# Boundary gathers from the input edge lists, with one short copied tail and a fixed first boundary list, in a three-layer edge convolution

## The chip, the cores and the metric

The kernel runs on one core of a Trainium2 chip. The metric is the device time of one launch in microseconds (us). The core has five engines that run beside each other and wait for one another by semaphores: TensorE (PE in the profile, PEld its weight loads), VectorE (DVE), ScalarE (ACT), GpSimd (POOL) and SyncE (SP). SP, ACT and POOL also issue DMAs; in the profile q1 is the queue of SP's DMAs, q10 that of ACT's and q0 that of POOL's, and all use the same 16 DMA engines.

## The reference

A layer norm and a relu, three edge convolutions over the same 80000 edges, and a product of all four feature sets, added to x:

```python
N, E = 2500, 80000                        # 256 features; dst is sorted
h = maximum(layernorm(x), 0)
xs = [h]
for W, b in ((W0, b0), (W1, b1), (W2, b2)):
    xi, xj = h[dst], h[src]
    m = concatenate([xi, xj - xi], -1) @ W + b
    s = segment_sum(m, dst, N)
    cnt = segment_sum(ones, dst, N)
    h = relu(s / maximum(cnt, 1)[:, None])
    xs.append(h)
return x + concatenate(xs, -1) @ Wf + bf
```

## The kernel before

The sum over edges is done as a product with a matrix of counts A, where A[s, d] is the number of edges from node s to node d. The kernel builds A once, from the edge lists, and multiplies it into the features in each layer. The nodes are taken in 20 tiles of 128 rows (ten pairs, numbered 0 to 9), and A's columns in windows of 6 destination nodes, 417 windows in 5 groups of up to 84.

**Finding the edges of a window.** Since dst is sorted, the edges of a window lie in a row. The kernel needs the place in the edge list at which each of 418 window boundaries lies; they stand in 4 blocks of 128 boundaries, one boundary on each partition. `dst` is loaded as `dst_i`, 128 rows of 625 edges. `find_first` takes the first entry of each row, `find_next` shifts it by one partition by a matmul, and `find_rows` makes `pick`, a 0/1 matrix that says in which row a boundary lies (`behind` is a step of it; `limr` holds the 512 boundaries as numbers, 6 apart). `pick_half` takes the right row of `dst_i` for each boundary by two matmuls per block, and `count_half` on ACT counts how many of the row's entries lie below the boundary. `search` makes of this the start `start_i` (six small DVE instructions), for block 0 alone and then for blocks 1 to 3 together. `get_edges` then reads, with two indirect DMAs on POOL, 256 entries of dst (`ed`) and of src (`es`) for each of a block's 128 boundaries, from that boundary's start on. A boundary's 256 entries serve the window ahead of it and the one behind it, so the first and last boundaries reach past the ends of the lists. For that the kernel copies both lists, at the start, into longer DRAM tensors `dst_e` and `src_e`, with 128 entries of `FAR` (a number above every node) ahead and behind, and gathers from those. The copies are two DMAs on ACT's queue and the borders two on SP's (lines 435 to 439).

**Counts.** `find_away` (ACT), `key_parts` and `key_high` (DVE, from `lo_i` on) make two keys of each edge, `key_turn` turns them by matmuls, `key_copy` (ACT) writes `key_m` and `key_n`. `compare` (DVE) makes 0/1 matrices `one_m` and `one_n` of the keys of 8 windows at once, `counts` (PE) multiplies them, and `take_counts` (ACT) writes the result into A's group. `degrees` and `shares` make the number of edges of a node, from `away`.

**Features.** For a pair q of tiles, `stats` (DVE) takes the layer norm's statistics of x, `spread`, `roots` and `scales` the scale and offset, `normalize` applies them on the engines that are named to it, `turn` (PE) and `take_turned` (ACT) transpose, and `product` (PE) multiplies by `W0` (names Z) and by `Wf` (names F). `split_high` (ACT) and `split_low` (DVE, writes `zl`) split the first product in two parts.

**What sets the order.** Up to the first layer, a table written by hand, `order`, lists these steps: a name is a function and its number (`Z6` is the product of pair 6 by `W0`, `st1` the statistics of pair 1, `ge0` the gather of block 0, `B5` a comparison, `Nm0` the normalization of pair 0 on DVE and ACT; `Nd` is both tiles on DVE, `Np` POOL and ACT, `Na` both on ACT, `N` both on POOL; `io` is `small_numbers`, `warm7` seven matmuls on zeros ahead of the next bank). The instructions of each engine are kept in this order, so a step that waits holds up what stands behind it on its engine. The loads of x stand in five chunks (pairs 0; 1 and 2; 3 to 5; 6 and 7; 8 and 9), all but the third on SP's queue. SP's and ACT's DMAs share eight completion semaphores in turn: a DMA waits until the one eight places ahead of it has landed. Then follow the first layer's groups, with the next group's counts woven in, and the second and third layers.

The recorded line of most instructions is 282, a helper that records them, so rows are told apart by their tiles.

Of the kernel before, what the change touches and what calls it, by code (L numbers as in the profile page):

```python
# [8 lines left out]
F32 = mybir.dt.float32  # L9
I32 = mybir.dt.int32  # L10
# [303 lines left out]
def by_windows(ctx: ExitStack, tc: tile.TileContext, x, src, dst, Ws, bs, Wf, bf, out, missing):  # L314
# [40 lines left out]
    assert W <= S - 2 and NT * S <= 256  # L355
    MORE = 4 - R % 4
# [50 lines left out]
    src_e, dst_e = (dram.tile([E + CAP, 1], I32, name=f"{z}_e") for z in ("src", "dst"))  # L407
# [26 lines left out]

    outer = pp.tile([CH, P], I32, name="outer")
    POOL.memset(outer, FAR)
    for long, of in ((dst_e, dst), (src_e, src)):
        ACTo.dma_start(long[P:P + E, :].rearrange("(p c) o -> p (c o)", p=P), of.rearrange("(p c) -> p c", p=P))
        SP.dma_start(bass.AP(tensor=long.tensor, offset=long.offset, ap=[[E + P, CH], [1, P]]), outer)
# [35 lines left out]

    lim_i = pp.tile([P, WG], I32, name="lim_i")
# [16 lines left out]
    load_b(1)  # L493
    DVE.memset(ones, 1.0)
# [3 lines left out]
    back = pp.tile([P, 2 * P], F32, name="back")  # L498
    POOL.memset(back, 0.0)
    POOL.tensor_copy(back[:, 1:P + 1], ident)  # L500
# [21 lines left out]
    limr = pp.tile([P, WG * P], F32, name="limr")  # L522
    first = pp.tile([P, 1], F32, name="first")
    after = pp.tile([P, 1], F32, name="after")
    behind = pp.tile([P, WG * P], F32, name="behind")
# [7 lines left out]
    edges = {}  # L533

# [6 lines left out]
    def limits():  # L541
        DVEo.tensor_copy(lim, lim_i)
        DVEo.tensor_copy(limr, limr_i)
        for h in range(CH):
            DVEo.tensor_scalar(below[:, h, :], lim, -1.0, 1.0 + (1 - h) * W, op0=OP.mult, op1=OP.add)
        DVEo.tensor_scalar(unlim, lim, -1.0, 0.5, op0=OP.mult, op1=OP.add)
# [35 lines left out]
    def search(i, j):  # L582
        sl = slice(i, j)
        DVEo.tensor_add(base[:, 0, sl], base[:, 0, sl], base[:, 1, sl])
        DVEo.tensor_scalar(end_f[:, sl], row[:, sl], float(R), float(HR + P * R - MORE), op0=OP.mult, op1=OP.add)
# [7 lines left out]
    def pick_starts(i, j):  # L593
# [3 lines left out]
        PEo.matmul(pe[:, :j - i], back[:, :P], end_f[:, i:j], start=True, stop=(i == 0))  # L597
        if i:
            PEo.matmul(pe[:, :j - i], back[:, P:], end_f[:, i - 1:j - 1], start=False, stop=True)
# [5 lines left out]
    def get_edges(i):  # L605

        edges[i] = [pp.tile([P, CAP], I32, name=f"e{z}{i}") for z in "sd"]
# [39 lines left out]
    def key_turn(i):  # L647
        pt = bank()
        for q, k in enumerate(parts[i]):
            for j in range(CH):  # L650
                PEo.matmul(pt[:, q * CAP + j * P:q * CAP + (j + 1) * P], k[:, j * P:(j + 1) * P], ident_b,
# [10 lines left out]
    def degrees(i):  # L662
# [17 lines left out]
        yield  # L680
        for m0 in range(0, min(P, NW + 1 - i * P), P // 2):
# [854 lines left out]
```

## Time and profile before

| what | value |
|---|---|
| time of the runs shown | median 471.64 us (471.01 to 471.9) |
| the profiled execution: time, span | 471.79 us, 470.0 us |
| granted clock of TensorE, mean | 0.99 |
| DMA moved over the span | 52.73 MB |

How to read the rows quoted below. A row of the timeline is: start (us), duration (us), engine, line, operation, tile written <- tiles read, shapes, count; in square brackets the time that the engine was idle before it and what ended that. "xN" merges N instructions that follow each other. A row of the stretches is: from and to, length, then the busy time of PE, PEld, DVE, ACT and POOL with the number of instructions, the granted clock of TensorE, the busy share of the DMA engines and GB/s. A row of a DMA queue is: packets, MB, and the time its packets took as a share of 16 engines. The layers' part of the profile looks like this, and stays as it is in all that follows:

```profile
L282 ACT CAST block<-staged 128x1008 fp32r<-128x1008 bf16 x120 | 118.0, 1031 | 16.5 <-DVE staged L282 6.9
L282 PE MATMUL bank<-block,zh 128*128 128x504 f32 (+1 forms) x200 | 83.8, 419 | 0.0
```

These are groups of like instructions, with the busy time (us), the mean of one (ns), and the idle time ahead of them.

### The profile page before, as it was taken

Reading aid. Unit: us, or ns where it says so; the run is one execution under the profiler, and the core shown is the slowest. Engines: PE = TensorE matmul, PEld = TensorE weight load, DVE = VectorE, ACT = ScalarE, POOL = GpSimd, SP = SyncE. Lnnn points to the kernel's source line nnn. Section 1 sums busy time; section 2 is a strip of 40 time slices with the busy share of each in tenths; the row PEclk is TensorE's granted clock in tenths of the full one; section 3 lists DMA queues with packets and bytes.
Section 4 is the critical chain, followed back from the end, with each engine's and each line's share of the span. In section 5 each row is a group of like instructions: output and inputs, shape, how many; then the busy total and the mean of one; then the engine's idle time right before and its main releaser. Section 6 shows DMA issues by size and latency. Waiting matters only on the chain.

```text
span 470.0 us, 7473 instructions
## 1 busy us (share of the span) xinstructions
PE 458.5 (98%) x2761; PEld 362.4 (77%) x2761; DVE 376.4 (80%) x721; ACT 312.1 (66%) x572; POOL 39.5 (8%) x65
## 2 busy tenths in 40 slices
PE   5999999999999999999999999999999999999995
PEld 2788887777777777878887877877788788688685
DVE  5889988889898873469988959876999687578795
ACT  2778769587664541387769857785787798497540
POOL 3473015200101001000000000000000000000000
PEclk9799999999999999999999999999999999999999
DMA  8510047990743708532178551010213955220014
GB/s 255 157 55 15 1 96 141 192 216 20 142 81 63 160 1 165 113 106 71 45 253 298 176 176 53 38 45 2 86 46 91 356 192 176 89 88 0 3 61 161
DMA packets 21785, 52.73 MB, mean 112 GB/s; under 512 B 1915, under 2 KB 12110, under 8 KB 21710
## 3 DMA queue, kind: packets, MB, share of 16 engines
q1 hardware_dynamic: 14318, 33.41, 21.1%
q0 software_dynamic: 5856, 16.51, 18.3%
q10 hardware_dynamic: 1568, 2.27, 1.6%
q8 instruction: 23, 0.38, 0.3%
q14 instruction: 20, 0.16, 0.1%
HBM read 36.72 MB, written 16.10 MB: 112 GB/s over the span
## 4 chain that ended last, share of the span: by engine, by line
PE 90%; ACT 3%; DVE 2%; issue 1%; DMA 1%; SPq 0%; POOL 0%; ACTq 0%; POOLq 0%; DVEq 0%
PE bank L282 84%; PE pz L282 6%; DMA acc<-in_x_dram 1%; ACT junk L282 1%; ACT a L282 1%; PE turned L282 1%; ACT hT L282 0%; ACT acc L282 0%; DVE one_m L282 0%; DVE own_h L282 0%; DVE one_n L282 0%; ACT zh L282 0%; DVE st L282 0%; DVE pick L282 0%; ACT away L282 0%
## 5 line engine op out<-in xcount | busy, mean ns | idle before, releaser
L282 ACT CAST block<-staged 128x1008 fp32r<-128x1008 bf16 x120 | 118.0, 1031 | 16.5 <-DVE staged L282 6.9
L282 PE MATMUL bank<-block,zh 128*128 128x504 f32 (+1 forms) x200 | 83.8, 419 | 0.0
L282 PE MATMUL bank<-a,zh 128*128 128x504 f32 (+1 forms) x200 | 81.9, 409 | 0.0
L282 PE MATMUL bank<-a,zl 128*128 128x504 f32 (+1 forms) x200 | 77.9, 390 | 0.0
L282 PE MATMUL bank<-block,zl 128*128 128x504 f32 (+1 forms) x200 | 77.3, 387 | 0.0
L282 ACT CAST a<-bank 128x480 fp32r<-128x480 f32 (+1 forms) x105 | 54.0, 561 | 32.4 <-PE bank L282 30.6
L282 DVE TENSOR_TENSOR one_m<-iota_m,key_m 128x2048 bf16<-128x2048 bf16 (+2 forms) x55 | 63.9, 1162 | 8.2 <-PE bank L282 7.9
L282 PE MATMUL bank<-block,sh 128*128 128x504 f32 x160 | 68.9, 430 | 0.0
L282 PE MATMUL bank<-block,staged 128*128 128x512 f32 (+1 forms) x288 | 62.8, 369 | 0.0
L282 PE MATMUL bank<-block,sl 128*128 128x504 f32 x160 | 62.6, 391 | 0.0
L282 PEld LDWEIGHTS bank<-block,staged 128*128 128x128 f32 x288 | 49.4, 188 | 10.1 <-issue 0.7
L282 DVE TENSOR_TENSOR block<-staged 128x1008 fp32r<-128x1008 bf16 x40 | 46.9, 1204 | 5.2 <-PE bank L282 3.9
L282 PEld LDWEIGHTS bank<-block,zh 128*128 128x128 f32 x200 | 37.6, 188 | 10.9 <-issue 2.5
L282 PEld LDWEIGHTS bank<-block,zl 128*128 128x128 f32 x200 | 37.6, 188 | 10.7 <-issue 3.2
L282 PEld LDWEIGHTS bank<-a,zh 128*128 128x128 f32 x200 | 37.9, 189 | 6.5 <-issue 0.2
L282 PEld LDWEIGHTS bank<-a,zl 128*128 128x128 f32 x200 | 37.8, 189 | 6.4 <-issue 0.2
L282 DVE TENSOR_TENSOR one_n<-iota_n,key_n 128x640 bf16<-128x640 bf16 (+2 forms) x110 | 42.4, 426 | 0.0
L282 PEld LDWEIGHTS <-one_m 128*128 128x128 bf16 x834 | 31.4, 98 | 13.9 <-issue 5.2
L282 PE MATMUL pz<-wbf,hT 128*128 128x256 f32 x160 | 40.7, 399 | 0.5 <-ACT hT L282 0.4
L282 PEld LDWEIGHTS bank<-block,sh 128*128 128x128 f32 x160 | 30.1, 188 | 10.3 <-issue 3.5
L282 PE MATMUL bank<-one_n,one_m 128*128 128x80 bf16 x834 | 37.6, 196 | 0.2
L282 PEld LDWEIGHTS bank<-block,sl 128*128 128x128 f32 x160 | 30.1, 188 | 9.4 <-issue 3.7
(172 smaller groups left out, 631.4 us busy)
## 6 DMA issues: line engine op xcount, KB each, us to landing
staged<-a_dram SPq DMA_DIRECT2D x52, 504.0 KB
a_dram<-a POOLq DMA_DIRECT2D x20, 630.0 KB, 8.3
acc<-in_x_dram POOLq DMA_DIRECT2D x3, 640.0 KB
out_dram<-acc SPq DMA_DIRECT2D x5, 256.0 KB
acc<-in_x_dram SPq DMA_DIRECT2D x2, 512.0 KB
wbf<-in_L_gnn_Wf_dram SPq DMA_DIRECT2D x4, 256.0 KB
acc<-in_x_dram ACTq DMA_DIRECT2D x1, 768.0 KB
wbf<-in_L_gnn_W_dram SPq DMA_DIRECT2D x3, 256.0 KB
```

The costliest lines, as they stand in the source:

```text
L282: return self.tc.keep_in_program_order(call(*args, **kwargs))
```

## The change

The full copies of the two lists go. Blocks 0, 1 and 2 gather straight from the inputs `dst` and `src`. Only the last block gathers from `dst_e` and `src_e`, of which only the last 20000 entries and a border of 128 behind them are written. Starts are held inside what each block may read by `least` and `most`, two small constant tiles that take the place of the constants 0 and E.

Block 0 now lists its boundaries in another way: its last partition holds boundary 0, whose entries are known beforehand (a border of fixed numbers and the first 128 edges, loaded by one DMA of one row for each list), and partitions 0 to 126 hold boundaries 1 to 127. So its gather has 127 partitions, and the matmuls that put the boundaries in order read `back_b` or `back` with a shift in block 0. `limr` in f32 goes; `find_rows` compares with the integer tile. The table `order` is another one.

```diff
-    lim = const.tile([P, WG], F32, name="lim")
-    back_b = const.tile([P, 2 * P], BF16, name="back_b")
+    back_b = const.tile([P, 2 * P + 1], BF16, name="back_b")
-    src_e, dst_e = (dram.tile([E + CAP, 1], I32, name=f"{z}_e") for z in ("src", "dst"))
+    TAIL = P // 4 * R
+    src_e, dst_e = (dram.tile([E + P, 1], I32, name=f"{z}_e") for z in ("src", "dst"))
-    outer = pp.tile([CH, P], I32, name="outer")
-    POOL.memset(outer, FAR)
-    for long, of in ((dst_e, dst), (src_e, src)):
-        ACTo.dma_start(long[P:P + E, :].rearrange("(p c) o -> p (c o)", p=P), of.rearrange("(p c) -> p c", p=P))
-        SP.dma_start(bass.AP(tensor=long.tensor, offset=long.offset, ap=[[E + P, CH], [1, P]]), outer)
...
-    POOLo.iota(lim_i, pattern=[[P * W, WG]], base=0, channel_multiplier=W)
+    POOLo.iota(line_i[:, 0:1], pattern=[[0, 1]], base=W, channel_multiplier=W)
+    POOLo.iota(lim_i[:, 1:], pattern=[[P * W, WG - 1]], base=P * W, channel_multiplier=W)
     POOLo.iota(limr_i, pattern=[[W, WG * P]], base=0, channel_multiplier=0)
+    POOLo.iota(limr_i[:, :P], pattern=[[W, P]], base=W, channel_multiplier=0)
+    POOLo.memset(limr_i[:, P - 1:P], 0)
...
+    outer = pp.tile([1, P], I32, name="outer")
+    POOL.memset(outer, FAR)
+    for k, (of, long, fill) in enumerate(((src, src_e, 0), (dst, dst_e, FAR))):
+        POOL.memset(edges[0][k][P - P // 4:, :P], fill)
+        SP.dma_start(edges[0][k][P - 1:, P:], of[0:P].rearrange("(o c) -> o c", o=1))
+        SP.dma_start(long[E - TAIL:E, :].rearrange("(p c) o -> p (c o)", c=R), of[E - TAIL:E].rearrange("(p c) -> p c", c=R))
+        SP.dma_start(long[E:, :].rearrange("c o -> o c"), outer)
...
+    POOL.memset(least[:, 1:], 0.0)
+    POOL.memset(least[:, WG - 1:], float(E - TAIL))
+    POOL.memset(most[:, :WG - 1], float(E - CAP))
+    POOL.memset(most[:, WG - 1:], float(E - P))
...
-        DVEo.tensor_copy(lim, lim_i)
-        DVEo.tensor_copy(limr, limr_i)
+        DVEo.scalar_tensor_tensor(lim_i[:, 0:1], line_i, float(P * W), line_i, op0=OP.is_lt, op1=OP.mult)
...
-        DVEo.tensor_scalar(behind, limr, after, None, op0=OP.is_gt)
-        DVEo.scalar_tensor_tensor(pick, limr, first, behind, op0=OP.is_gt, op1=OP.subtract)
+        DVEo.tensor_scalar(behind, limr_i, after, None, op0=OP.is_gt)
+        DVEo.scalar_tensor_tensor(pick, limr_i, first, behind, op0=OP.is_gt, op1=OP.subtract)
...
-        DVEo.tensor_scalar(end_f[:, sl], end_f[:, sl], float(E), 0.0, op0=OP.min, op1=OP.max)
-        DVEo.tensor_copy(start_i[:, sl], end_f[:, sl])
+        DVEo.tensor_tensor(end_f[:, sl], end_f[:, sl], most[:, sl], op=OP.min)
+        DVEo.tensor_tensor(start_i[:, sl], end_f[:, sl], least[:, sl], op=OP.max)
...
-        for t, of in ((ed, dst_e), (es, src_e)):
+        n = P - (i == 0)
+        for t, of in ((ed, dst_e if i == WG - 1 else dst.rearrange("(e o) -> e o", o=1)),
+                      (es, src_e if i == WG - 1 else src.rearrange("(e o) -> e o", o=1))):
             POOLo.indirect_dma_start(
-                out=t, out_offset=None, in_=of,
-                in_offset=bass.IndirectOffsetOnAxis(ap=start_i[:, i:i + 1], axis=0))
+                out=t[:n, :], out_offset=None, in_=of,
+                in_offset=bass.IndirectOffsetOnAxis(ap=start_i[:n, i:i + 1], axis=0))
...
-        warm7 lim io first next dstr st0 rs0 sq0 pick sc0 warm8 Nm0 pk00 sg00 pk01 st1 T0 pk11 R0 sg01 st2 rs1 sq1 Z0
+        warm7 lim first next dstr st0 io rs0 pick warm8 st1 sq0 sc0 Nd0 pk01 pk00 sg01 sg00 st4 T0 pk11 R0 rs1 sq1 pk30
```

On SyncE, at the program's start, `acc` is the tile that x is loaded into, `wbf` and `wt` are weights, `outer` the border. Before:

```order
L439 DMA dst_e<-outer 2x128
L439 DMA src_e<-outer 2x128
L282 DMA acc<-in_x_dram 128x2x256
L282 DMA acc<-in_x_dram 128x4x256
L282 DMA wbf<-in_L_gnn_W_dram 128x2x256
```

And after the change, with the rows that follow the loads of x and the weights:

```order
L282 DMA acc<-in_x_dram 128x2x256
L282 DMA acc<-in_x_dram 128x4x256
L282 DMA wbf<-in_L_gnn_W_dram 128x2x256
L282 DMA acc<-in_x_dram 128x4x256
L282 DMA wbf<-in_L_gnn_Wf_dram 128x2x256
L282 DMA acc<-in_x_dram 128x3x256
L282 DMA acc<-in_x_dram 68x256
L282 DMA wt<-in_L_gnn_W_dram 128x2x256
L498 DMA es_160<-in_src_dram 1x128
L489 DMA brow<-in_L_gnn_b_dram 1x256 x2
L499 DMA src_e<-in_src_dram 16x1250
```

The loads of x move to the head of SyncE's queue, and everything for the edge lists stands behind them. On ScalarE's queue the two copies that stood between `dst_i` and x's third chunk are gone.

On VectorE, from the first statistics (`st`, of the tiles in `acc`) to the start numbers of block 0 (`base`, `end_f`), before:

```order
L282 BN_STATS st<-acc 128x6 x2
L282 BN_AGGR mv<-st 128x2 x2
L282 TENSOR_SCALAR rs<-mv 128x2
L282 TENSOR_TENSOR after<-bank,after 128x1
L282 TENSOR_SCALAR behind<-limr,after 128x512
L282 SCALAR_TENSOR_TENSOR pick<-limr,first,behind 128x512
L282 RECIPROCAL rs<-rs 128x2
L282 SCALAR_TENSOR_TENSOR off<-mv,rs 128x2
L282 TENSOR_SCALAR acc<-acc,rs,off 128x256
L282 BN_STATS st<-acc 128x6 x2
L282 BN_AGGR mv<-st 128x2 x2
```

After the change:

```order
L282 CAST iota_m<-im_i 128x128
L282 CAST iota_n<-im_i 128x20x6
L282 CAST nc__102<-nc_i 128x8
L282 TENSOR_SCALAR rs<-mv 128x2
L282 TENSOR_TENSOR after<-bank,after 128x1
L282 TENSOR_SCALAR behind<-limr_i,after 128x512
L282 SCALAR_TENSOR_TENSOR pick<-limr_i,first,behind 128x512
L282 BN_STATS st<-acc 128x6 x2
L282 BN_AGGR mv<-st 128x2 x2
L282 RECIPROCAL rs<-rs 128x2
L282 SCALAR_TENSOR_TENSOR off<-mv,rs 128x2
L282 TENSOR_SCALAR acc<-acc,rs,off 128x256 x2
```

Three small casts now stand between the first statistics and `pick`, and a second pair's statistics and a second normalization stand ahead of the first transposes.

On GpSimd, around the first gather (`ed` and `es` are the gathered lists), before:

```order
L501 CAST back_b<-back 128x256
L282 DMA ed_303<-dst_e,start_i 128x256
L282 DMA es_302<-src_e,start_i 128x256
L282 TENSOR_SCALAR acc<-acc,rs,off 128x256 x6
L282 DMA ed_446<-dst_e,start_i 128x256
```

After the change:

```order
L542 MEMSET least 128x1
L282 TENSOR_SCALAR acc<-acc,rs,off 128x256
L282 DMA ed_161<-in_dst_dram,start_i 127x256
L282 DMA es_160<-in_src_dram,start_i 127x256
L282 TENSOR_SCALAR acc<-acc,rs,off 128x256 x5
L282 DMA ed_163<-in_dst_dram,start_i 128x256
```

One normalization moves ahead of the gather, and the gather reads the inputs with 127 partitions.

More of the change, by code (lines that the diff above doesn't have):

```diff
@@ L493, in by_windows @@
     load_b(1)
+    edges = {i: [pp.tile([P, CAP], I32, name=f"e{z}{i}") for z in "sd"] for i in range(WG)}
+    outer = pp.tile([1, P], I32, name="outer")
[5 more added lines that the diff above has]
+        SP.dma_start(long[E:, :].rearrange("c o -> o c"), outer)
     DVE.memset(ones, 1.0)
@@ L497, in by_windows @@
     POOL.tensor_copy(ident_b, ident)
-    back = pp.tile([P, 2 * P], F32, name="back")
-    POOL.memset(back, 0.0)
-    POOL.tensor_copy(back[:, 1:P + 1], ident)
+    back = pp.tile([P, 2 * P + 1], F32, name="back")
+    POOL.memset(back[:, 0:1], 0.0)
+    POOL.tensor_copy(back[:, 1:].rearrange("p (k n) -> p k n", k=2), ident.unsqueeze(1).to_broadcast([P, 2, P]))
     POOL.tensor_copy(back_b, back)
@@ L517, in warmed @@
         return to
-    limr = pp.tile([P, WG * P], F32, name="limr")
     first = pp.tile([P, 1], F32, name="first")
     after = pp.tile([P, 1], F32, name="after")
-    behind = pp.tile([P, WG * P], F32, name="behind")
+    behind = pp.tile([P, WG * P], BF16, name="behind")
     pick = pp.tile([P, WG * P], F32R, name="pick")
@@ L532, in by_windows @@
     start_i = pp.tile([P, WG], I32, name="start_i")
-    edges = {}
+    least = pp.tile([P, WG], F32, name="least")
+    most = pp.tile([P, WG], F32, name="most")
+    POOL.memset(least[:, 1:], 0.0)
+    POOL.memset(least[:, WG - 1:], float(E - TAIL))
+    POOL.memset(most[:, :WG - 1], float(E - CAP))
+    POOL.memset(most[:, WG - 1:], float(E - P))
     def small_numbers():
@@ L596, in pick_starts @@
         ends_before.append(pe)
[L597 to L599 removed]
+        PEo.matmul(pe[:, :j - i], back[:, 0 if i else P:][:, :P], end_f[:, i:j], start=True, stop=(i == 0), skip_group_check=True)
+        for k in range(i, j) if i else ():
+            PEo.matmul(pe[0:1, k - i:k - i + 1], back[:, P - (k == 1):][:, :1], end_f[:, k - 1:k], start=False, stop=(k == j - 1),
+                       skip_group_check=True)
     def set_starts(i, j):
@@ L680, in degrees @@
         yield
+        here, before = (ident_b, back_b) if i else (back_b[:, P:], back_b[:, P - 1:])
         for m0 in range(0, min(P, NW + 1 - i * P), P // 2):
```

32 lines of the change are left out of this document (17 added, 15 removed).

## The prediction

> **What bounds the kernel now.** I read the page first (engines, chain), then the busy time by stretches, then the timeline of the first 65 us, and last the DMA queues of the first 12 us.
>
> ```profile
> span 470.0 us, 7473 instructions
> PE 458.5 (98%) x2761; PEld 362.4 (77%) x2761; DVE 376.4 (80%) x721; ACT 312.1 (66%) x572; POOL 39.5 (8%) x65
> 0.00:10.00 10.00, 6.18 (x17) 2.40 (x17) 4.63 (x24) 2.29 (x4) 3.90 (x18) 1.00 0.79 236
> 10.00:20.00 10.00, 8.31 (x30) 6.82 (x31) 8.89 (x44) 6.41 (x21) 2.17 (x2) 0.66 0.78 248
> 20.00:30.00 10.00, 9.97 (x58) 8.82 (x57) 8.67 (x35) 6.36 (x18) 6.88 (x10) 1.00 0.10 28
> 30.00:60.00 30.00, 29.84 (x285) 25.81 (x284) 29.55 (x57) 24.68 (x56) 8.90 (x11) 1.00 0.07 19
> ```
>
> TensorE (PE) is busy for 98% of the span, and from 20 us on for all but a few tenths of each stretch. So what is left to win lies before 20 us, and a microsecond won there is kept only if PE stays full behind it. In the last row VectorE (DVE) is as full as PE, 29.55 of 30 us: it must move forward too. The third number from the right, the granted clock, is 0.66 in the second stretch. What PE waits for at the start:
>
> ```profile
> 8.31 0.75 DVE L282 BATCH_NORM_STATS2 st<-acc 128x6 f32<-128x256 f32 x2 [4.17 <-DMA acc<-in_x_dram]
> 10.10 0.75 DVE L282 SCALAR_TENSOR_TENSOR pick<-limr,first,behind 128x512 fp32r<-128x512 f32 x1
> 11.00 0.86 PE L282 MATMUL bank<-dst_r,pick 128*128 128x314 f32 x2 [3.19 <-DVE rs L282]
> 13.43 3.78 PE L282 MATMUL pz<-wbf,hT 128*128 128x256 f32 x8 [0.43 <-ACT hT L282]
> 18.50 1.89 PE L282 MATMUL pz<-wbf,hT 128*128 128x256 f32 x8
> 25.40 1.99 PE L282 MATMUL pz<-wbf,hT 128*128 128x256 f32 x8
> ```
>
> DVE idles 4.17 us until the first chunk of x has landed (8.31); the pick numbers for the edge search stand behind its statistics and are done at 10.86; PE starts at 11.00. Its first product takes 3.78 us, the next 1.89 us: half speed, then full. I use the product at 25.40 (tile pair 6, on `Wf`) as the milestone, since from there PE's list is nearly the same in both kernels.
>
> **The change part by part.** *The copies.* Who issues what, and what the queues moved:
>
> ```profile
> 0.83 0.40 ACTq L282 DMA_DIRECT2D dst_i<-in_dst_dram  x1
> 1.26 0.61 ACTq L282 DMA_DIRECT2D dst_e<-in_dst_dram  x1
> 1.91 0.60 ACTq L282 DMA_DIRECT2D src_e<-in_src_dram  x1
> 0.95 0.32 SPq L439 DMA_DIRECT2D dst_e<-outer  x1
> 1.61 1.13 SPq L282 DMA_DIRECT2D acc<-in_x_dram  x2
> q10 hardware_dynamic: 197, 0.90, 51.5%
> q1 hardware_dynamic: 244, 0.24, 12.8%
> DMA packets 749, 0.74 MB, mean 371 GB/s; under 512 B 25, under 2 KB 749, under 8 KB 749
> q10 hardware_dynamic: 111, 0.35, 124.8%
> 3.88 0.15 DVE L282 CAST first<-dst_i 128x1 f32<-128x1 int32 x1
> ```
>
> The first two queue rows are for 0 to 6 us: ScalarE's queue q10 had moved 0.90 MB, the list `dst_i` (0.32) and most of the two full copies, and SyncE's q1 only 0.24 MB. x's first chunk is 0.26 MB, so its bytes were through shortly after 6 us, and DVE saw it 2.2 us later. The row of packets is for 9.5 to 11.5 us, with both queues on rows of 1 KB: 371 GB/s. After the change q10 carries `dst_i` and then x's third chunk, q1 has x at its head, issued at 0.95 instead of 1.61. The last queue row is for 2 to 3 us, in which q10 moved what `dst_i` holds. With the first bytes at about 2.1 (an estimate from that row), `dst_i`, x's first chunk and what q10 sends beside it (0.77 MB) take 2.1 us: 4.2 us, to 4.6 if q10 has the larger share. Landing trailed the bytes by 0.9 us (`dst_i`: done by 3.0, used at 3.88) to 2.2 us. So the chunk lands between 5.1 and 6.8 us; I take 5.9, **2.4 us sooner**. The other x chunks come sooner by more than that and are never last.
>
> *DVE up to the gather.* Unit prices:
>
> ```profile
> 2.70 0.41 DVE L282 CAST iota_m<-im_i 128x128 bf16<-128x128 int32 x1
> 3.00 0.37 DVE L282 CAST iota_n<-im_i 128x120 bf16<-128x120 int32 x1
> 11.16 0.41 DVE L282 TENSOR_SCALAR acc<-acc,rs,off 128x256 f32<-128x256 f32 x1
> 15.12 0.74 DVE L282 BATCH_NORM_STATS2 st<-acc 128x6 f32<-128x256 f32 x2
> 16.00 0.72 DVE L282 BATCH_NORM_STATS2 st<-acc 128x6 f32<-128x256 f32 x2
> 21.80 0.53 DVE L282 TENSOR_SCALAR lo_i<-es 128x256 int32<-128x256 int32 x1
> ```
>
> A pair of tiles costs 0.87 us of statistics (start to start, 15.12 to 16.00). The three small casts (`io`) move from DVE's idle time to behind the first statistics: 0.3 us from start to start, 0.7 for the three. The two casts of the limits go, out of idle time: nothing. `behind` now reads int32 and writes bf16; no row shows that pair, but DVE reads int32 in 0.53 us for 256 elements at worst (`lo_i`) and f32 in 0.41, so the ends are 0 and +0.25, and I take 0. Minimum and maximum by `most` and `least` replace two instructions of the same small shape: 0. So pick ends at 5.9 + 0.87 + 0.7 + 0.2 + 1.28 = 8.95 instead of 10.86. Behind it the new order puts statistics of pair 1 (0.87), the scale (0.35) and two normalizations on DVE instead of one (0.4 each): the first pair is ready for PE at 10.95, against the 11.57 of before. Statistics of pair 4 (0.87), the start numbers (seven instructions of 0.15 us, as the small cast at 3.88: 1.05), a scale (0.35): 13.2. Five more pairs (4.35), numbers and a scale (0.6), one more pair (0.87), `zl` (0.7): `lo_i` at 19.8 instead of 21.80, with one pair and one normalization more behind it, so DVE has gained 2.0 + 0.87 + 0.4 = 3.3 us.
>
> *The gather of boundary block 0* stands behind a normalization of 0.6 us on POOL and reads the input itself; nothing of it waits for a copy any more, only for the one row that SyncE loads, which is issued behind x. It is issued at 13.85 and 15.3, against 15.01 and 16.50.
>
> ```profile
> 15.01 1.19 POOL L282 DMA_INDIRECT ed<-dst_e,start_i  x1 [10.40 <-DVE rs L282]
> 16.50 0.98 POOL L282 DMA_INDIRECT es<-src_e,start_i  x1 [0.30 <-issue]
> 32.80 1.03 POOL L282 DMA_INDIRECT ed<-dst_e,start_i  x1 [0.16 <-issue]
> 4.21 0.40 POOL L501 CAST back_b<-back 128x256 bf16<-128x256 f32 x1
> es<-src_e,start_i POOLq DMA_INDIRECT x1, 2.8
> q0 software_dynamic: 22, 0.09, 83.2%
> ```
>
> The fifth row, of the DMA issues from 15 to 20 us: 2.8 us from issue to landing for `es`, so it lands at 18.1, before `lo_i` asks for it (19.8). If that cover goes, each microsecond past 19.8 stands on DVE with the statistics of pair 3, the start numbers of three blocks and the first comparison queued behind. The copy of the last 20000 edges (0.16 MB) runs on q1 behind all of x; the last block was gathered at 32.80: 0. POOL's added memsets and iotas end about 1.2 us after the 4.6 us of before, still ahead of what reads them: 0, at worst 0.3 us where the casts of `io` share that time.
>
> *PE.* Its first real work starts at 9.0 instead of 11.00. How fast it runs is open:
>
> ```profile
> 4.87 2.94 PE L282 MATMUL bank<-idle 128*128 128x512 bf16 x8
> 7.04:10.45 3.41, 0.77 (x4) 0.15 (x2) 2.03 (x8) 0.20 (x1) 0.00 (x0) 1.00 1.02 322
> 10.45:13.86 3.41, 2.43 (x8) 1.95 (x9) 2.84 (x13) 2.23 (x8) 0.00 (x0) 0.50 1.10 352
> 13.86:17.27 3.41, 3.41 (x9) 2.66 (x9) 3.18 (x18) 1.76 (x6) 1.96 (x2) 0.50 0.86 265
> ```
>
> The granted clock fell to 0.50 at 10.45, behind a stretch in which PE was busy for 0.77 of 3.41 us (the warming matmuls end at 7.81), and came back at 17.27, behind a full stretch; 2.43 of 3.41 was not enough. After the change the first of these stretches holds the end of the warming (0.8) and two to three pick matmuls (0.5): some 1.4 of 3.41 us, which no row has. The two ends: at full clock the first product runs 11.9 to 13.65, the next pair's 14.4 to 16.15, the two behind it to 18.15 and 20.4; then normalizations on POOL (last at 21.3) and ScalarE's list are late next, and the milestone comes at 22.8, **2.6 us sooner**. At half clock up to 17.27 the first product ends at 15.65, the second at 18.85, the others at 20.85 and 23.1, the milestone at 24.3: **1.1 us sooner**. I take the middle, 1.8, since 1.4 lies between the rows that fell (0.77) and held (full).
>
> The Trainium skill (TensorE: Matmul & The Clock Gate, "What you observe" and "What's actually happening") says the clock is judged in free-running windows of 3413 ns, that a busy one frees it and an idle one halves it. The trace agrees on the length: 10.45 to 17.27 is twice 3.41. Taken at its word 1.4 us of work is not an idle window, and the gain would be 2.6 us; the row with 0.77 us, which fell, says that idle need not mean empty, and leaves 1.1 us possible.
>
> *Behind the milestone.*
>
> ```profile
> 27.85 0.68 DVE L282 TENSOR_TENSOR one_m<-iota_m,key_m 128x1024 bf16<-128x1024 bf16 x1
> ```
>
> DVE waits for the first keys, compares them from 24.8 instead of 27.85, but has 1.2 us of work to catch up that was done by then before (`sc4`, `zl` of pair 1, `lead`): it is about 1.6 us ahead at 30 us, and has 0.45 us of idle time up to 60 to give. That supports 1.8 as well. From 64 us on the order is the same.
>
> *Sum.* The profiled execution took 471.79 us, 470.0 of it span and 1.8 around it, 0.15 above the median of the runs shown (471.64). 471.79 - 1.8 = 470.0; against the median 469.8. **I forecast 469.9**, by the clock's ends 469.1 to 470.7.
>
> **The rivals.** The row of q1 up to 4 us:
>
> ```profile
> q1 hardware_dynamic: 10, 0.00, 0.4%
> ```
>
> *More than that.* x's chunk lands at 4.5, `dst_i` beside it, and the full clock holds: 2.6 + 1.4 = 4.0 us, 467.7. For it: 371 GB/s and 0.9 us of trailing. Against it: DVE is full behind 30 us.
>
> *No difference.* The chunk is late for another reason than the copies: q1 had moved next to nothing by 4 us although it was issued at 1.61. Then only the 0.66 us of earlier issue count, the casts and the statistics put ahead of the first normalization (0.7 + 0.87 + 0.4) eat them, and the milestone lies at 24.6 to 25.6: 470.9 to 472.0, say 471.6. Against it: q1 speeds up exactly as the copies end. This is also the case in which the change does not do what it says.
>
> *Slower: the gather of 127 rows.* The first block now gathers 127 partitions, a number that 16 engines can't share evenly. In the row of q0 (27.5 to 28 us) 22 packets, nearly all of 4 KB, took 83.2% of 16 engines for half a microsecond: 0.30 us each. If the 127 rows of 1 KB were worked through by one engine, that is 32 packets, 9.7 us instead of the 0.6 us of 16 engines; `es` lands at 15.3 + 2.8 + 9.1 = 27.2, `lo_i` is 7.4 us late, the keys reach PE at 29.2 and the milestone comes at 29.6, 4.2 us later than now: 476.0. It decides from a landing at about 23.4 on, since up to there the 2.6 us won and 1.1 us of slack at the milestone pay for it. Against it: block 1 to 3 show gathers of 128 rows only, nothing of 127.
>
> The Trainium skill (DMA: Bandwidth & Descriptors, "Why a DMA increments its semaphore by 16 and not by 1") states that rule: the number of engines is the largest up to 16 that divides the slowest dimension, and 127 partitions go to one; it excepts some direct copies from POOL, which get all 16. No run here shows which holds for this gather.
>
> **How the numbers follow.** Forecast 0.58, more 0.08, no difference 0.20, slower 0.14. A measurement of this kernel tells about 0.2% (0.9 us) from no change. So faster 0.66, same 0.20, slower 0.14. The range takes in the clock's ends, the better case and the case of no difference with what the casts and int32 might add: 467.7 to 472.6. It leaves out the slow gather.
>
> **What would show it.** The first statistics start at about 5.9 (below 6.8); pick ends near 9; the first product's eight matmuls take 1.7 to 1.9 us or 3.8; `lo_i` starts near 19.8 and its idle time does not name the gather; the milestone product, the first after the keys' transposes, starts at 22.8 to 24.3; q10 moves only 1.1 MB in the first 12 us. The prediction is wrong if x lands after 7.5, if DVE waits for `es` or `ed`, or if PE, though earlier at 25 us, is found waiting for comparisons between 30 and 64 us.

## The result, and the profile after

| kernel | median | against the kernel before |
|---|---|---|
| before | 471.32 us (4 runs, 470.63 to 471.9) | |
| changed | 475.80 us (4 runs, 474.93 to 476.62) | ratio 1.0094, interval [1.0077, 1.0111] |

The change makes the kernel 4.5 us slower. The forecast was 469.9 us, with 467.7 to 472.6 as its range; the time lies outside of it. It is that of the rival "the gather of 127 rows" (476.0), which had a chance of 0.14.

The page of the changed kernel, its head and its engines, and the busy time by the same stretches as before (from and to, length, busy time of PE, PEld, DVE, ACT and POOL, granted clock, DMA share, GB/s):

```profile
span 474.8 us, 7504 instructions
PE 461.0 (97%) x2765; PEld 363.1 (76%) x2765; DVE 375.0 (79%) x723; ACT 313.2 (66%) x573; POOL 40.8 (9%) x72
```

```profile
0.00:10.00 10.00, 7.98 (x22) 3.55 (x23) 6.62 (x34) 2.92 (x6) 4.12 (x27) 1.00 0.83 264
10.00:20.00 10.00, 9.46 (x47) 7.73 (x45) 8.27 (x42) 5.95 (x22) 6.84 (x5) 1.00 0.55 153
20.00:30.00 10.00, 4.40 (x16) 2.67 (x17) 3.25 (x17) 5.20 (x15) 1.79 (x4) 0.68 0.09 23
30.00:60.00 30.00, 30.00 (x256) 26.20 (x255) 27.30 (x59) 22.53 (x52) 10.43 (x12) 0.93 0.10 28
```

Compare stretch by stretch. From 10 to 20 us PE is busier than before (9.46 against 8.31) and at full clock (1.00 against 0.66): there the change works. From 20 to 30 us PE falls from 9.97 to 4.40 and VectorE from 8.67 to 3.25, and the clock is 0.68. A hole of more than 5 us has opened where before there was none.

The timeline of the changed kernel, the rows that answer to those of before:

```profile
5.01 0.75 DVE L282 BATCH_NORM_STATS2 st<-acc 128x6 f32<-128x256 f32 x2
7.07 0.75 DVE L282 SCALAR_TENSOR_TENSOR pick<-limr_i,first,behind 128x512 fp32r<-128x512 int32 x1
11.35 1.99 PE L282 MATMUL pz<-wbf,hT 128*128 128x256 f32 x8
13.37 2.80 POOL L282 DMA_INDIRECT ed<-in_dst_dram,start_i  x1 [0.21 <-issue]
16.47 2.58 POOL L282 DMA_INDIRECT es<-in_src_dram,start_i  x1 [0.30 <-issue]
24.25 0.69 ACT L282 ACTIVATE away<-ed,below 128x128 bf16<-128x128 int32 x2 [6.87 <-DMA ed<-in_dst_dram,start_i]
26.33 0.29 DVE L282 TENSOR_SCALAR lo_i<-es 128x256 int32<-128x256 int32 x1 [7.51 <-DMA es<-in_src_dram,start_i]
28.19 3.77 PE L282 MATMUL pz<-wbf,hT 128*128 128x256 f32 x8
```

Read it from the top. The statistics start 3.3 us sooner (5.01 against 8.31), `pick` ends at 7.82 instead of 10.86, and the first product starts 2.1 us sooner and takes 1.99 us instead of 3.78. Then ScalarE waits 6.87 us for `ed` and VectorE 7.51 us for `es`, the two gathers of block 0. The milestone product starts at 28.19 (before 25.40) and takes twice as long. The waits by engine, up to 30 us (total, times, longest):

```profile
DVE lo_i L282 <- DMA es<-in_src_dram,start_i: 7.5, 1, 7.5
ACT away L282 <- DMA ed<-in_dst_dram,start_i: 6.9, 1, 6.9
PEld turned L282 <- ACT acc L282: 3.4, 1, 3.4
```

The third row is how the wait reaches PE: ScalarE's normalization of `acc` stands in its order behind `away`, which waits for `ed`, and PE wants to transpose that `acc`. Behind it PE also waits for the keys, which are made from `es` (0.94 and 0.49 us at 27.12 and 28.00). The DMA issues and queue of the gathers, from 13.3 to 27 us (us from issue to landing; packets, MB, share of 16 engines), of the changed kernel:

```profile
q0 software_dynamic: 1056, 0.28, 10.7%
ed<-in_dst_dram,start_i POOLq DMA_INDIRECT x1, 10.8
es<-in_src_dram,start_i POOLq DMA_INDIRECT x1, 9.8
```

And of the kernel before, the same stretch, which also holds two gathers:

```profile
q0 software_dynamic: 96, 0.26, 6.7%
```

The same bytes went in 1056 packets instead of 96, and landed after 10 us instead of 2.8.

### The profile page after: what moved, and what is told of

It is laid out like the page before. It is cut to its first block, busy times and chain, and to the rows that moved or that the text cites. A ratio compares the mean times of both kernels' runs of the same rounds, so it can differ in the third digit from the quotient of the medians.

```text
span 474.8 us, 7504 instructions
## 1 busy us (share of the span) xinstructions
PE 461.0 (97%) x2765; PEld 363.1 (76%) x2765; DVE 375.0 (79%) x723; ACT 313.2 (66%) x573; POOL 40.8 (9%) x72
## 4 chain that ended last, share of the span: by engine, by line
PE 93%; DMA 3%; issue 1%; POOL 1%; DVE 0%; SPq 0%; POOLq 0%; DVEq 0%
PE bank L282 86%; PE pz L282 7%; DMA es<-in_src_dram,start_i 2%; DMA acc<-in_x_dram 1%; PE turned L282 1%; POOL ed L282 1%; POOL acc L282 0%; DVE acc L282 0%; SPq L282 0%; DVE kn L282 0%; DVE lo_i L282 0%; DVE away L282 0%; DVE room L282 0%; DVE es L282 0%; DVE fewer L282 0%
## 5 line engine op out<-in xcount | busy, mean ns | idle before, releaser
L282 PEld LDWEIGHTS <-one_m 128*128 128x128 bf16 x834 | 31.3, 98 | 13.3 <-issue 4.6
## 6 DMA issues: line engine op xcount, KB each, us to landing
acc<-in_x_dram POOLq DMA_DIRECT2D x3, 640.0 KB, 11.9
```

Of the source, the lines that this page charges most:

```text
L282: return self.tc.keep_in_program_order(call(*args, **kwargs))
```

## The experiments

There were two questions: is it the number 127, or something else about the new gather; and what made x late before. "Late row" below means one edit, which the other kernels build on: block 0's gather gets 128 rows again. Boundary 0's row is gathered too, from any valid start, and the fixed row is then copied over it from a small tile. The medians come from more than one chip, so kernels are best compared by their ratio to the kernel before, which ran beside each of them. A trace is of one execution.

**128 rows, the fixed row behind the gather** (g128_late_row). Against the changed kernel:

```diff
-        SP.dma_start(edges[0][k][P - 1:, P:], of[0:P].rearrange("(o c) -> o c", o=1))
+        fix.append(pp.tile([1, CAP], I32, name=f"fix{k}"))
+        SP.dma_start(fix[k][:, P:], of[0:P].rearrange("(o c) -> o c", o=1))
...
+            DVEo.tensor_scalar(start_0, start_i[:, 0:1], 0, None, op0=OP.max)
...
-        n = P - (i == 0)
+        n = P
...
+            SP.dma_start(ed[P - 1:, :], fix[1])
+            SP.dma_start(es[P - 1:, :], fix[0])
```

> The changed kernel, but block 0 gathers 128 rows again (the start of boundary 0, which lies 128 entries ahead of the list, is raised to 0 for the gather by one more small VectorE instruction), and the fixed row is written over row 127 afterwards by one DMA of one row for each list. Theory G (the gather of 127 rows is what is slow, for its number of rows): ed and es land about 3 us after their issue instead of 10.8 and 9.8, lo_i waits only for the late row, 1 to 2 us instead of 7.5, POOL spends about 1.0 to 1.2 us on each issue instead of 2.8, and the time is 468.5 to 470.5 us. Theory C (the first gather is slow because it reads the inputs while the tail copies and x's last loads run): ed and es still take 9 us or more, time 475 to 476.5. Theory O (the new order loses the time): lo_i no longer waits, but the time stays above 473.

467.52 us, ratio to the kernel before 0.9932 [0.9913, 0.9951]: faster than both kernels, and a microsecond below the range expected of the number of rows. Its timeline:

```profile
13.53 1.20 POOL L282 DMA_INDIRECT ed<-in_dst_dram,start  x1 [0.18 <-issue]
19.62 0.35 DVE L282 TENSOR_SCALAR lo_i<-es 128x256 int32<-128x256 int32 x1 [0.61 <-DMA es<-fix]
21.99 1.99 PE L282 MATMUL pz<-wbf,hT 128*128 128x256 f32 x8 [0.28 <-ACT hT L282]
```

POOL issues the gather in 1.20 us instead of 2.80, `lo_i` starts at 19.62 (the prediction had 19.8), and the milestone stands at 21.99, 3.4 us sooner than before. The row copied behind the gather costs VectorE 0.61 us of waiting (and ScalarE 0.85). Its busy time by stretches shows no hole, and full clock throughout:

```profile
10.00:20.00 10.00, 9.83 (x50) 8.22 (x49) 8.71 (x45) 7.63 (x27) 5.06 (x8) 1.00 0.53 149
20.00:30.00 10.00, 9.52 (x73) 8.03 (x71) 8.71 (x32) 7.77 (x22) 6.11 (x7) 1.00 0.23 68
30.00:60.00 30.00, 30.00 (x283) 26.42 (x281) 29.71 (x57) 24.03 (x54) 6.80 (x10) 1.00 0.08 20
```

**The same with 127 rows** (g127_late_row). Only the number goes back:

```diff
-        n = P
+        n = P - (i == 0)
```

> Like g128_late_row in everything, with the fixed row still loaded into tiles of its own and copied to partition 127, but the gather of block 0 has 127 rows again. If the number of rows is what makes the changed kernel slow: ed and es land some 10 us after they are issued, the first lo_i starts at 26 to 27 with 6.5 to 7.5 us of idle time named after es's gather, the clock falls to 0.50 between 24 and 33, and the time is 475 to 476.5. If the gain of g128_late_row came from another part of its edit (the fixed row out of the way of the gather, the start tile of its own): 467 to 468.5, and no wait for the gather.

476.98 us (475 to 476.5 was expected), ratio 1.012 [1.009, 1.0149]. The wait is back, in the waits up to 30 us:

```profile
DVE lo_i L282 <- DMA es<-in_src_dram,start: 8.1, 1, 8.1
```

So one row fewer costs 9.5 us by the medians (476.98 - 467.52, both on the same chip), 8.9 by the two ratios; and at 127 rows the late-row edit is no faster than the changed kernel (475.80), so the number of rows is what it gained by.

**Gathers of other sizes, one by one** (rows_by_number). In the kernel g128_head_copy, told of below, seven more gathers of `dst` with 128 to 64 rows, which nothing needs, each followed by a small copy on POOL that waits for it, at 42 us, where POOL and its queue are idle:

```diff
+        for n in more:
+            POOLo.indirect_dma_start(
+                out=more[n][:n, :], out_offset=None, in_=dst.rearrange("(e o) -> e o", o=1),
+                in_offset=bass.IndirectOffsetOnAxis(ap=start_i[:n, 1:2], axis=0))
+            POOLo.tensor_copy(seen[:n], more[n][:n, 0:1])
```

> The head-copy kernel with seven extra gathers of 256 entries per row from dst, for 128, 127, 126, 124, 120, 112 and 64 rows, one after the other on POOL behind its last normalization, each followed by a small POOL copy that waits for its landing; nothing uses them, and the time of this kernel says nothing but what they cost. Theory G, split by the largest divisor up to 16 (16, 1, 14, 4, 15, 16 and 16 engines): 128, 112, 64, 120 and 126 rows about 3 us from issue to landing, 124 rows 4 to 5, 127 about 10. If only multiples of 16 are handled whole, 126, 124 and 120 are as slow as 127. Theory C: all seven take about 3 us, 127 too.

The whole took 484.96 us, which is compared with nothing, as the gathers are extra work. The times between the issue and the copy, on POOL's timeline:

```profile
42.63 0.97 POOL L282 DMA_INDIRECT rows<-in_dst_dram,start_i  x1 [0.15 <-issue]
45.52 0.19 POOL L282 COPY seen<-rows 128x1 int32<-128x1 int32 x1 [1.92 <-DMA rows<-in_dst_dram,start_i]
45.90 3.58 POOL L282 DMA_INDIRECT rows<-in_dst_dram,start_i  x1 [0.19 <-issue]
56.91 2.00 POOL L282 COPY seen<-rows 127x1 int32<-127x1 int32 x1 [7.44 <-DMA rows<-in_dst_dram,start_i]
59.10 1.01 POOL L282 DMA_INDIRECT rows<-in_dst_dram,start_i  x1 [0.18 <-issue]
62.09 1.12 POOL L282 COPY seen<-rows 126x1 int32<-126x1 int32 x1 [1.98 <-DMA rows<-in_dst_dram,start_i]
```

128 rows take 2.9 us, 127 take 11.0, 126 take 3.0. In the rows that follow these, 124, 120, 112 and 64 take 4.8, 3.8, 2.8 and 2.6. Each was taken once. It isn't that 16 must divide the number: 126 is fast. The largest divisors up to 16 are 16 for 128, 1 for 127, 14 for 126, 4 for 124, 15 for 120, 16 for 112 and 64, and but for 120 the times go by them. The packets do too: the 126 rows went in 28 packets of more than 2 KB, 14 of 0.5 to 2 KB and 22 small ones, which is what 14 engines make of nine rows of 1 KB each (twice 4 KB and once 1 KB). The queue of POOL for the 127 rows, first from 45.9 to 57 us, then from 52.5 to 56 us:

```profile
q0 software_dynamic: 528, 0.14, 6.5%
q0 software_dynamic: 20, 0.08, 6.4%
```

The first row is an average over unlike parts. POOL was at the issue until 49.48, and no packet moved before 50. From 50 to 52 us 493 packets of less than 512 B went by beside the first data; what they are for, the profile doesn't say. Then only data is left, the second row: 20 packets of 4 KB in 3.5 us, at 6.4% of 16 engines, which is 1.02 engines. That is one engine at work, with 0.18 us for a packet. So of the 8.1 us that 127 rows take longer than 128, 2.6 are POOL's longer issue (3.58 against 0.97), and most of the rest is the data going through one engine: for 128 rows 46 of the 48 packets went within 1 us.

The Trainium skill (DMA: Bandwidth & Descriptors, "Why a DMA increments its semaphore by 16 and not by 1") gives this rule, with 127 partitions on one engine, and an exception for some direct copies from POOL. The trace agrees that the rule holds for an indirect gather from POOL: 11.0 us against 2.9, with the data at 1.02 engines.

**Without late row: copy the head of the lists** (g128_head_copy, g128_head_sync). Block 0 gets 128 gathered rows in another way: a copy of the first 30000 entries with a border ahead of it, from which block 0 gathers. First on ScalarE's queue, behind x, then the same on SyncE's:

```diff
+    for long, of in ((dst_h, dst), (src_h, src)):
+        ACTo.dma_start(long[P:P + HEAD, :].rearrange("(p c) o -> p (c o)", c=R), of[0:HEAD].rearrange("(p c) -> p c", c=R))
+        ACTo.dma_start(long[0:P, :].rearrange("c o -> o c"), outer)
```

> The changed kernel with the fixed row taken away: block 0 gathers 128 rows, boundary 0's among them, from a copy of the first 30000 edges with a border of 128 ahead (two copies of 0.12 MB on ScalarE's queue behind x's third chunk, and one more small VectorE instruction for the start). Theory G: ed and es land about 3 us after issue, lo_i does not wait, the first layer's products start about 3 us sooner than in the kernel before, time 467.5 to 469.5. Theory C: still 9 us or more, 475 to 476.5. Theory O: no wait, but above 473. A wait of ed's issue for the copies, if they land after 13 us, would add what it shows.

471.99 us, ratio 1.0021 [1.0009, 1.0032], where 467.5 to 469.5 was expected. `lo_i` waits for no gather, but ScalarE waits for 10.27 us. Its timeline, the last two of its DMAs and what stands next:

```profile
4.85 0.50 ACTq L282 DMA_DIRECT2D src_h<-in_src_dram  x1
10.02 0.22 ACTq L282 DMA_DIRECT2D src_h<-outer  x1
10.27 1.28 ACT L282 ACT_TABLE_LOAD   x1 [10.27 <-DMA src_h<-in_src_dram]
```

The last DMA of six was issued only at 10.02, and all that ScalarE computes stood behind it; PE's pick matmuls started at 12.42 and the clock fell. The expectation had left out that a DMA that must wait holds up the compute of the engine that issues it.

> g128_head_copy with its four DMAs (copies of the first 30000 entries and their borders) on SyncE's queue behind all of x and the first weights, instead of ScalarE's. If ScalarE's blocked instruction stream was what g128_head_copy lost by: no ACT idle time named after src_h, first product at 11.3 to 11.6 in 2.0 us, and 467.3 to 469 (as g128_late_row, or up to 1.5 us more where the copies land behind 13.4 and hold the gather up). If not the stream but the bytes of the copies were to blame: first product later than 12.5 again, 470 or more.

467.73 us, ratio 0.9931 [0.9904, 0.9958]. With the same bytes on SyncE, which computes nothing, the loss is gone. The bytes also go later there, behind all of x; but they hadn't made x's first chunk late in g128_head_copy either, where the first statistics start at 4.86. That leaves two forms with 128 rows, without and with a copy, both 3.2 to 3.4 us faster than before.

**The order table** (old_copies_new_order, g128_late_old_order). The kernel before with the new table, and late row with the old one; each edit only replaces the table.

> The kernel before, with its full copies and its gathers of 128 rows, and the changed kernel's order table. It tells what the order does by itself. Theory G: x still lands at about 8.3, the casts and the second statistics stand ahead of the first normalization, so 471 to 473. Theory O: 474.5 or more, most of the loss.

471.11 us, ratio 1.0005 [0.9992, 1.0018].

> g128_late_row with the order table of the kernel before. If the table is worth as little here as in old_copies_new_order: 467.2 to 468.2. If the new table is what turns the earlier x into time (a second pair's statistics and normalization ahead of the first transposes, one normalization ahead of the gather): 468.5 to 470, with the milestone product a microsecond or more behind 22.0.

468.54 us, ratio 0.9938 [0.9913, 0.9964], its interval over that of late row. The median lies in the range that was given for a table that matters (468.5 to 470), but the milestone is at 22.23, 0.24 us behind late row, and not the microsecond expected with it. The table changes nothing that can be told here, in neither kernel.

**What made x late** (g128_late_copies, g128_late_borders, g128_late_both, g128_borders_only, g128_borders_copies). Late row, with the DMAs that the change removed put back, into tensors that nobody reads: the two copies on ScalarE's queue, the two borders on SyncE's ahead of x, or both:

```diff
+    for long, of in ((dst_x, dst), (src_x, src)):
+        ACTo.dma_start(long[P:P + E, :].rearrange("(p c) o -> p (c o)", p=P), of.rearrange("(p c) -> p c", p=P))
+        SP.dma_start(bass.AP(tensor=long.tensor, offset=long.offset, ap=[[E + P, CH], [1, P]]), outer_x)
```

> g128_late_row with the two full copies of the edge lists put back on ScalarE's queue behind dst_i, into tensors that nobody reads. If the copies held up x, as the prediction has it: x's first chunk lands near 7.5 to 8.3 (SyncE still has x at the head of its queue), pick ends about 2.5 us later than 7.8, the first product runs at half speed (3.8 us), and the time is 470.5 to 472. If x was late in the kernel before because its loads stood behind the borders on SyncE's queue and not because of the copies: first statistics at 5 to 5.7 and 467.3 to 468.3.

470.59 us, ratio 0.9993 [0.9978, 1.0009]: nearly the whole gain is gone, but not in the way expected. VectorE's statistics in that kernel:

```profile
5.12 0.42 DVE L282 BATCH_NORM_STATS2 st<-acc 128x6 f32<-128x256 f32 x1
12.78 0.75 DVE L282 BATCH_NORM_STATS2 st<-acc 128x6 f32<-128x256 f32 x2 [2.97 <-DMA acc<-in_x_dram]
```

The first chunk of x is there as early as without the copies (5.12 against 5.10 in late row). It is the third chunk that the copies hold back: it stands behind them on ScalarE's queue, issued at 2.53 instead of 1.24, and the new table takes a pair of it (`st4`) as the third statistics (they start at 10.37 in late row, 2.4 us sooner). The second product then runs at half clock. So the copies alone did not make the first chunk late. Whether they would cost as much with the old table, which takes pair 4 later, no run shows.

> g128_late_row with only the two border DMAs of the kernel before put back on SyncE's queue ahead of x, without the copies. If being issued 0.66 us later is what made x late in the kernel before: first statistics at 7.5 to 8.3, 470 to 471.5. If the copies must be there too, since x then falls in behind them: x is 0.6 us later than in g128_late_row and no more, first statistics at 5.5 to 6, 467.5 to 468.5.

470.89 us, ratio 1.0003 [0.9989, 1.0017], the first statistics at 7.21. Here the fixed row's load had also come to stand ahead of x on SyncE's queue, so that x was issued at 1.73. The next kernel has SyncE's loads as they were, only with the borders ahead.

> g128_late_borders again, but without the fixed row's load that had come to stand ahead of the borders there: SyncE's queue is the two borders, then x; ScalarE's is dst_i, then x's third chunk; no copies. x's first chunk is issued at 1.5 to 1.7, as in the kernel before, behind 0.95 MB that ScalarE has queued by 1.3. If who issues first decides who moves first: first statistics at 6.5 to 7.5 and 469.5 to 471.5. If it needed the extra load (issue at 1.73): first statistics at 5.5 to 6 and 467.5 to 468.5.

471.08 us, ratio 1.0 [0.9989, 1.0011]. First statistics of this kernel:

```profile
7.24 0.75 DVE L282 BATCH_NORM_STATS2 st<-acc 128x6 f32<-128x256 f32 x2 [3.17 <-DMA acc<-in_x_dram]
```

Its two queues up to 5 us:

```profile
q10 hardware_dynamic: 710, 0.90, 61.1%
q1 hardware_dynamic: 8, 0.00, 0.2%
```

And those of g128_late_row up to 5 us, where x is issued at 0.73 instead of 1.61:

```profile
q1 hardware_dynamic: 533, 0.53, 36.6%
q10 hardware_dynamic: 166, 0.34, 19.4%
```

With x issued 0.9 us later its statistics start 2.1 us later: ScalarE's queue, which was given `dst_i` at 0.81 and x's third chunk at 1.22, moved 0.90 MB first, and SyncE's only 8 packets, all before 3.5 us. Two borders of 1 KB each ahead of x are enough for that. Two causes are not separated here: x is issued later, and it stands behind the borders on its own queue. No run has one without the other.

> g128_late_row with the two copies and the two borders of the kernel before, unread, in the kernel before's order on both queues. If the two together make x late: first statistics at 8 to 8.5, the first product at half speed, and 470.5 to 472, about what g128_late_copies gave although there the first chunk landed at 5.1. If the copies alone set the time, whatever stands ahead of x: within 0.5 of g128_late_copies (470.6) and first statistics below 6.

472.87 us, ratio 1.0028 [1.0016, 1.0039], again with the fixed row's load ahead; the first statistics start at 7.64. Without it:

> g128_borders_only with the two unread copies on ScalarE's queue as well: both queues begin as in the kernel before, with everything else as in g128_late_row. If the start of the two queues is all that the change gained by: first statistics at 7.5 to 8.5, first product at half speed, 471 to 473, so not faster than the kernel before. If other parts of the change (block 0's new list, the order, the casts that went) gain by themselves: below 470.

471.38 us, ratio 1.0011 [0.9999, 1.0023], with the first statistics at 7.86. The four kernels with 128 rows that differ in these DMAs are:

| on the queues | first statistics | median | ratio to the kernel before |
|---|---|---|---|
| neither (g128_late_row) | 5.10 | 467.52 us | 0.9932 |
| copies (g128_late_copies) | 5.12 | 470.59 us | 0.9993 |
| borders (g128_borders_only) | 7.24 | 471.08 us | 1.0 |
| both (g128_borders_copies) | 7.86 | 471.38 us | 1.0011 |

Either alone costs nearly all of it, and the second adds almost nothing. (7.24 and 7.86 can't be told apart: the kernel before and old_copies_new_order have the same DMAs at the head of both queues, and their first statistics start at 8.31 and 7.17.) The clock shows a part of it. Busy time in two adjoining stretches of 3.41 us, of g128_late_copies:

```profile
13.01:16.42 3.41, 1.50 (x9) 0.77 (x7) 3.17 (x20) 1.85 (x7) 1.04 (x2) 1.00 0.59 161
16.42:19.83 3.41, 3.41 (x10) 2.80 (x10) 3.34 (x19) 1.84 (x6) 1.69 (x2) 0.50 0.35 101
```

Of g128_borders_only, in three:

```profile
5.20:8.61 3.41, 1.70 (x8) 0.59 (x6) 1.38 (x9) 0.00 (x0) 0.00 (x0) 1.00 1.08 363
8.61:12.02 3.41, 0.88 (x5) 0.53 (x5) 3.20 (x15) 1.48 (x6) 0.00 (x0) 1.00 1.10 349
12.02:15.43 3.41, 3.25 (x10) 2.48 (x10) 3.17 (x20) 2.34 (x8) 0.98 (x2) 0.50 0.45 129
```

In each there is a stretch in which PE has too little to do (1.50 and 0.88 us), behind which it runs at half clock for 3.41 us; behind the stretch with 1.70 us the clock held. Of the four kernels only the one without copies and borders keeps 1.00 from the start. (That the wait and the clock together make the 3 us is argued from these rows and not shown; no run held the clock up while x was late. The profiled execution of g128_borders_only was the shortest of its ten, 470.05 us.)

## Why the prediction was wrong

**The step that failed** is "the gather of boundary block 0": issued at 13.85 and 15.3, landing at 18.1 by the 2.8 us of the gather before, ahead of `lo_i` at 19.8, cost 0. The issues came at 13.37 and 16.47, the second 1.2 us late as POOL was held 2.80 us by the first; then the landing took 9.8 us and came at 26.3. The 2.8 us were the row of a gather with 128 rows; with 127 they hold no more. The prediction named this, priced it, and gave it 0.14, with one argument against it: that no row shows a gather of 127. That is no evidence. The rule spoke of just this number, nothing in the trace spoke against it, and the only doubt was an exception for another kind of DMA. That rival should have been the likeliest, or close to it.

**Its price came out right by errors that cancel, which is luck.** It had 9.7 us on one engine, a landing at 27.2, `lo_i` 7.4 us late and the milestone at 29.6, 4.2 us later than before. Measured: a landing at 26.3, VectorE idle for 7.5 us at `lo_i`, the milestone at 28.19, and a span 4.8 us longer. So its milestone was 1.4 us too late, and 2.0 us more were lost behind the milestone. Within the gather, too, its 32 packets at 0.30 us each were too dear (0.18 us for the 127 rows of rows_by_number), while POOL's longer issue was missing: `es` landed 9.8 us behind its issue instead of 11.9, but that issue came 1.2 us later than forecast. In the profiled executions the rest of the change gains 4.4 us (span 470.0 to 465.6 in g128_late_row) and the gather loses 9.2 (465.6 to 474.8), where the rival had 2.6 and about 7; by the ratios to the kernel before it is 3.2 and 7.6. What it lacked on the side of the loss is the clock, of the changed kernel in stretches of 3.41 us:

```profile
20.27:23.68 3.41, 1.31 (x6) 0.60 (x6) 0.00 (x0) 0.00 (x0) 1.52 (x3) 1.00 0.19 47
23.68:27.09 3.41, 0.69 (x2) 0.29 (x2) 0.72 (x3) 2.60 (x8) 0.00 (x0) 0.50 0.04 13
27.09:30.51 3.42, 2.91 (x10) 2.15 (x11) 3.04 (x16) 2.69 (x8) 0.48 (x1) 0.50 0.02 5
30.51:33.92 3.41, 3.41 (x12) 2.76 (x11) 3.17 (x9) 1.07 (x3) 2.80 (x3) 0.50 0.14 38
```

PE worked 0.69 + 2.91 + 3.41 = 7.0 us at half speed, which is some 3.5 us of work lost, if all of it went at half the rate. Its idle time up to 40 us is 8.2 us, against 2.8 in late row: 5.4. The sum is 8.9 of the 9.2 us.

**x's first chunk: right in sign, wrong in cause.** It was there by 5.01 at the latest (forecast 5.9, bounds 5.1 to 6.8). But "the copies" were named as the reason, and with the copies it lands as early. With the borders alone it is late (7.24): it is then issued 0.9 us later, behind them and behind what the other queue had issued already. Which of these holds it up stays open. The rival "no difference" was wrong too in counting the earlier issue as 0.66 us and no more.

**The clock at the start: full, so the better end, for a reason the prediction did not have.** The middle value of 1.8 us was too small, the milestone came 3.4 us sooner in late row (forecast 2.6 at full clock). The term was mis-sized because the stretch was expected to hold 1.4 us of PE's work; it held far more, as PE's timeline of the changed kernel shows:

```profile
5.19 0.56 PE L282 MATMUL bank<-first,shift 128*128 128x1 f32 x2 [0.39 <-DVE first L282]
5.61 3.57 PE L282 MATMUL bank<-idle 128*128 128x512 bf16 x8
8.62 1.09 PE L282 MATMUL bank<-dst_r,pick 128*128 128x314 f32 x2
```

`dst_i` comes later beside x, so the second row of warming matmuls, behind the two that read `first`, runs from 5.61 instead of 4.87 and reaches up to the pick matmuls: PE has no gap there and is busy for all of the 3.41 us from 6.62 on. The prediction asked whether 1.4 of 3.41 us holds the clock. By the rows above it doesn't: 0.88, 1.31 and 1.50 let it fall, and 1.70 held it. The Trainium skill (TensorE: Matmul & The Clock Gate, "What's actually happening") lets the clock fall behind an idle window; in these traces a window with 1.50 of 3.41 us of work is idle enough for that.

**VectorE up to the gather, int32 in `behind`, POOL's memsets: near, in part by luck.** `pick` ended at 7.82, 1.1 us sooner than forecast, as x was 0.9 sooner and the three small casts took 0.3 us instead of 0.7 (5.90 to 6.21); `behind` took 0.49 us, as before. Yet `lo_i` starts at 19.62 with 128 rows, against 19.8: VectorE waits 0.56 us for x's third chunk at 10.37, where the prediction had said that the other chunks are never last, and 0.61 us for the copied row. PE's gain is kept behind the milestone, as was asked: late row has 30.00 of 30 us busy from 30 to 60.

## What to carry to other kernels

Look at the number of partitions of every DMA that a change touches, and prefer one with a large divisor up to 16: here giving up one row of 128 cost 9.5 us, more than twice all that the change gained, 126 rows were as fast as 128, and copying the missing row on afterwards cost 0.6 us of waiting. Put first on its queue what the first engine waits for, and look at what the other queue issues in the same microsecond. Where a gain hangs on keeping the clock up, the prices of two causes need not add: here each of two cost nearly the whole gain when it alone was put back.

## What the runs showed of the hardware

- A gather of 127 rows from POOL took 11.0 us, of 126 rows 3.0 and of 128 rows 2.9. It also made 528 packets instead of 48, of which 32 of more than 2 KB in both cases, and held POOL itself for 2.6 to 3.6 us instead of 1.0 to 1.2 at its issue.
- The granted clock fell behind stretches of 3.41 us in which PE was busy for up to 1.50 us (in that one, of g128_late_copies, PE's longest wait was 1.11 us), and held behind 1.70 (g128_borders_only) and 1.94 (g128_head_copy, from 5.39). It came back behind 3.25 us, but not behind 2.91 (the stretch from 27.09 above); in g128_late_both it came back behind 2.83 (from 15.17), so the busy time that the profile shows for a stretch does not decide that alone.
- Two queues did not share the DMA engines evenly: in g128_borders_only, with ScalarE's DMAs issued from 0.81, SyncE's borders from 0.95 and its x from 1.61 on, q1 moved 8 packets in the first 5 us and q10 710. The engines need not have been full: in the kernel before, from 3.5 to 4 us, q10 had a share of 15.9% and q1 of 1.8%, though x had been issued by 2.74. What kept x back is open; no run tells.
